# A state space layer's schedule: eight decay tiles, one copy for two, and steps moved by a few turns

## The chip, the cores and the metric

The kernel runs on one core of a Trainium2 chip. The metric is device time in microseconds (us). The core has a matrix engine (TensorE, PE in the profile), a vector engine (VectorE, DVE), an activation engine (ScalarE, ACT), a general engine (GpSimd, POOL) and a queue engine (SyncE, SP) that issues most of the DMAs. Each of them works through its own instructions in their program order, and waits at an instruction until what it needs is there; a weight load (PEld) can run ahead of PE's matmuls.

## The reference, cut to what matters

The whole model is a metaformer of four layers on an input of 4 x 64 x 128 x 128. The change lies in the convolution part of its third layer (layer 2), a state space layer followed by an MLP. For each of 4 batches it sees 64 channels and 8192 positions (image row w, channel c):

```python
xn = layer_norm(xf) over the 64 channels          # mu, var, rsqrt, ln_g, ln_b
xz = in_proj(xn); xi, z = split(xz)               # 128 each
xs = silu(causal_conv4(xi) + conv_b)
dt, Bm, Cm = split(x_proj(xs))                    # 4, 16 and 16 rows
dt = softplus(dt_proj(dt) + dt_proj_b)            # 128 rows
# for every position t, inner channel d and state s of 16:
h[d, s] = exp(dt[t, d] * A[d, s]) * h[d, s] + dt[t, d] * xs[t, d] * Bm[t, s]
y[t, d] = sum_s h[d, s] * Cm[t, s] + xs[t, d] * D[d]
out = out_proj(y * silu(z))                       # 64 channels
# over the last axis of 128:
result = fc2(gelu(fc1(out) + fc1_b)) + fc2_b      # 128 -> 512 -> 128
```

The layer's input is normed once more ahead of it, over the last axis, and its result is added to the input (the residual).

## The kernel before, in words

`l2_conv` (line 2353) goes through 64 **chunks**: two pairs of batches, and in each pair 32 groups of four image columns, L = 512 positions. A chunk has T = 32 **units**: two batches times 16 states. In a unit the 128 partitions hold two states of 64 inner channels, and its work is

- `decay` (ACT, L2821): da = exp(dt * A), one 128 x 512 activation, into one of five buffers;
- `spread` (PE, L2831, once for two units): a matmul with a one-hot matrix repeats two rows of Bm over the partitions, into one of four PSUM banks;
- `inputs` (DVE, L2865): dx * spread rows, into a PSUM bank;
- `one_state` (DVE, L2873): the scan h = da * h + input along the 512 positions; then on POOL (L2878) the product gs with the row of Cm, which DMA has repeated over the partitions (`fetch`);
- `summed` (PE, L2889, for two units, five units later): the sum over the states, accumulated in `py`.

Units 16 and 17 of a chunk are "apart": their da lies in a PSUM bank, and POOL makes their input.

The order on PE, ACT, DVE and POOL is written by hand. A loop runs over **turns** t, one for each unit. A turn emits the decay and the spread of unit t + 3, the input of unit t + 1, the scan of unit t, then all steps that `at(turn, ...)` has put down for this turn, then `summed` of unit t - 5. Each engine keeps this order; SP's order alone is left to the framework. The steps belong to three groups, each with a start turn t0 that is a multiple of 32:

- `norm(n, T * (n - 2))`, the norm over channels of chunk n, two chunks ahead: `scale` (ACT), `centre` (PE, matmul into the bank `pn`, L2544), `square` (ACT: a copy and a square, L2547 and L2548), `mean2` (PE, four matmuls of two columns, L2553), `root` (ACT), `newton` (POOL, four small ones), `back` (PE, 16 matmuls as the trace counts them, L2572), `kept` (ACT, a copy, L2578), `done` (POOL, L2585 and L2586).
- `project(n, T * (n - 1))`, one chunk ahead: `conv` (PE, 4 steps), `conv_out` (ACT, L2630), `gate_in` (PE, L2636), `gate_out` (ACT, L2639), `silu` (ACT with two table loads, L2645 and L2473), `bcr` (PE, x_proj, L2651), `bcr_out` (ACT: bt in bf16, bc and r, L2655 to L2657), `minus` and `part` (PE and ACT, which leave the bf16 rest of Bm in further rows), `steps` (PE, dt_proj, L2677), then softplus: `parts`, `exp`, `one_more`, `log` on ACT, `lost`, `add_lost`, `size`, `scaled` on POOL (L2696 to L2713), and `twice`, DMAs on SP that put dt and dx into the units' layout. `load_res` fetches the residual.
- `leave(n, T * (n + 1))`, the chunk after: `sums` (DVE, L2745), `project_out` and `projected`, `layer1` (PE, L2758), `hidden` (ACT, L2763), `gelu` (ACT with two table loads), `layer2` (PE: bias with a one-row matmul, residual with the identity, then eight products in two steps; L2774 to L2777), `put` (ACT, a copy L2784, and the store), each for the two batches 0 and 1 of the pair.

`centre`, `mean2`, `back`, `project_out` and `layer2` share one PSUM bank, `pn`: each of them waits until the one before has been read. `conv`, `gate_in`, `bcr`, `steps` and `layer1` share the two-bank tile `pa` in the same way. Once in four chunks (`statistics`), DVE takes the first norm's statistics of 16 columns, POOL merges them at turn 24 (v, L2504), ACT takes the root at turn 26 (L2508), and POOL makes rs16 and nb at turn 28 (up to L2520), which `scale` needs at turn 30.

Of the kernel before, what the change touches and what calls it, by code (L numbers as in the profile page):

```python
# [2352 lines left out]
def l2_conv(env, x, out, prm):  # L2353
# [15 lines left out]
    with ExitStack() as ctx:  # L2369
# [7 lines left out]
        def load(name, shape, src):  # L2377
            t = cp.tile(shape, F32, name=name)
            nc.sync.dma_start(t, src)
            return t  # L2380
# [54 lines left out]
        nc.vector.tensor_scalar(minus_i, env.ident[0 : 2 * N, 0 : 2 * N], -1.0, None, ALU.mult)  # L2435
        both = cp.tile([P, H], F32, name="both")
        nc.vector.tensor_add(both, env.ident[:, 0:H], env.ident[:, H:P])
        dtw = load("dtw", [R, D], prm["dt_proj_wT"])
        dtb = load("dtb", [P, 1], prm["dt_proj_b"].unsqueeze(1))
        am = cp.tile([P, S // 2, 2], F32, name="am")  # L2440
        for i in range(2):
# [27 lines left out]
        def at(turn, *steps):  # L2469
            turns.setdefault(turn, []).extend(steps)  # L2470
# [58 lines left out]
        def norm(n, t0):  # L2529
            g, w0 = chunks[n]  # L2530
            x_ = boxes[n]

            def scale(js):
                r, k = x_["rows"]
                if 0 in js:
                    tile_of(x_, "xn", [P, 3 + L], bufs=3)
                for j in js:
                    nc.scalar.activation(
                        x_["xn"][:, 3 + j * C : 3 + j * C + C], r["xt"][:, k + j, :], AF.Identity,
                        bias=r["nb"][:, k + j : k + j + 1], scale=r["rs16"][:, k + j : k + j + 1],  # L2540
                    )

            def centre():
                nc.tensor.matmul(tile_of(x_, "pm", [P, L], "pn", 1, pool=p1), less, x_["xn"][:, 3:], start=True, stop=True)  # L2544

            def square():
                nc.scalar.copy(x_["xn"][:, 3:], x_["pm"])  # L2547
                nc.scalar.activation(tile_of(x_, "sq", [P, L], "sq", 1), x_["pm"], AF.Square)  # L2548

            def mean2():  # L2550
                pv = tile_of(x_, "pv", [P, NW, 2], "pn", 1, pool=p1)
                for q in range(NW):
                    nc.tensor.matmul(pv[:, q, :], x_["sq"][:, q * C : q * C + C], each, start=True, stop=True)  # L2553

            def root():
                v, rs = tile_of(x_, "v", [P, NW, 2]), tile_of(x_, "rs", [P, NW, 2])
                nc.scalar.activation(v, x_["pv"], AF.Identity, bias=env.eps5)
                nc.scalar.activation(rs, v, AF.Ln)
                nc.scalar.activation(rs, rs, AF.Exp, scale=-0.5)

            def newton():
                v, rs, t = x_["v"], x_["rs"], tile_of(x_, "r2", [P, NW, 2])
                nc.gpsimd.tensor_tensor(t, rs, rs, ALU.mult)
                nc.gpsimd.tensor_tensor(t, t, v, ALU.mult)
                nc.gpsimd.tensor_scalar(t, t, 0.5, -1.5, ALU.mult, ALU.add)
                nc.gpsimd.tensor_tensor(rs, rs, t, ALU.mult)

            def back():
                pr = tile_of(x_, "pr", [P, L], "pn", 1, pool=p1)
                for q in range(NW):  # L2570
                    for b in range(2):
                        nc.tensor.matmul(  # L2572
                            pr[b * H : b * H + H, q * C : q * C + C], x_["rs"][:, q, b : b + 1].to_broadcast([P, H]),
                            env.ident, start=True, stop=True,
                        )

            def kept():
                nc.scalar.copy(tile_of(x_, "rt", [P, L], bufs=1), x_["pr"])  # L2578

            def done():  # L2580
                xn = x_["xn"]
                if w0 == 0:
                    nc.gpsimd.memset(xn[:, 0:3], 0.0)
                else:
                    nc.gpsimd.tensor_copy(xn[:, 0:3], boxes[n - 1]["xn"][:, L : L + 3])  # L2585
                nc.gpsimd.tensor_tensor(xn[:, 3:], xn[:, 3:], x_["rt"], ALU.mult)  # L2586

            at(t0 - 2, lambda: scale((0, 1)))
            at(t0, lambda: scale((2, 3)))
            at(t0 + 3, centre)  # L2590
            at(t0 + 4, square)
            at(t0 + 5, mean2)
            at(t0 + 6, root)
            at(t0 + 8, newton)
            at(t0 + 11, back)
            at(t0 + 12, kept)
            at(t0 + 13, done)


        def project(n, t0):  # L2600
# [52 lines left out]
            def bcr_out():  # L2653
                ps = x_["ps"]
                nc.scalar.copy(tile_of(x_, "bt", [3 * N, 2, L], dt=BF16), ps[0 : 3 * N])  # L2655
                nc.scalar.copy(tile_of(x_, "bc", [2 * N, 2, L], bufs=1), ps[0 : 2 * N])
                nc.scalar.copy(tile_of(x_, "r", [R, 2, L], bufs=1), ps[3 * N : 3 * N + R])  # L2657

            def c_out():
                for b in range(2):  # L2660
# [13 lines left out]
            def steps():  # L2674
                pu = tile_of(x_, "pu", [P, 2, L], "pa", 1, pool=pa)
                for b in range(2):
                    nc.tensor.matmul(pu[:, b, :], dtw, x_["r"][:, b, :], start=True, stop=True)  # L2677

            def parts():
                pu = x_["pu"]  # L2680
# [32 lines left out]
                nc.gpsimd.tensor_tensor(x_["dx"], x_["dt"], x_["xs"], ALU.mult)  # L2713

            for k in range(4):
                at(t0 - 8 + k, lambda k=k: conv(k))
            at(t0 - 4, conv_out)
            at(t0 - 2, gate_in)
            at(t0 - 1, gate_out)
            at(t0 + 1, silu)  # L2720
            at(t0 + 7, lambda: bcr(0))
            at(t0 + 8, lambda: bcr(1))
            at(t0 + 9, bcr_out, c_out)
# [15 lines left out]
        def leave(n, t0):  # L2739
# [12 lines left out]
            def projected(b):  # L2752
                nc.scalar.copy(tile_of(x_, "o%d" % b, [P, NW * H], bufs=1), x_["po"].rearrange("c w h -> c (w h)"))
# [11 lines left out]
            def gelu():  # L2765
# [2 lines left out]
                    nc.scalar.activation(gl, gl, AF.Gelu)  # L2768
                base_table()

            def layer2(b, q):
                if q == 0:
                    tile_of(x_, "p2%d" % b, [P, NW // 2, C], "pn", 1, pool=p1)
                    nc.tensor.matmul(x_["p2%d" % b], one_row, b2, start=True, stop=False)  # L2774
                    nc.tensor.matmul(x_["p2%d" % b], env.ident, x_["res%d" % b], start=False, stop=False)
                for k in range(F):
                    nc.tensor.matmul(  # L2777
                        x_["p2%d" % b][:, q, :], x_["gl%d" % b][:, k, q * P : q * P + P], f2[:, k, :],
                        start=False, stop=(q == 1 and k == F - 1),
                    )  # L2780
# [7 lines left out]

            at(t0 - S + LAG, lambda: sums(0))
            at(t0 + LAG, lambda: sums(1))  # L2790
            at(t0 + 9, lambda: project_out(0))
            at(t0 + 10, lambda: projected(0))
            at(t0 + 13, lambda: project_out(1))
            at(t0 + 14, lambda: projected(1))
            at(t0 + 18, lambda: layer1(0))
            at(t0 + 19, lambda: hidden(0))
            at(t0 + 21, lambda: layer1(1))
            at(t0 + 22, lambda: hidden(1))
            at(t0 + 24, gelu)
            at(t0 + 28, lambda: layer2(0, 0))  # L2800
            at(t0 + 29, lambda: layer2(0, 1))
            at(t0 + 30, lambda: put(0))
            at(t0 + 31, lambda: layer2(1, 0))
            at(t0 + 32, lambda: layer2(1, 1))
            at(t0 + 33, lambda: put(1))


        def unit(t):
# [8 lines left out]

        def decay(t):
            x_, b, s, _ = unit(t)
            da = bank(t, t % 2) if apart(t) else sb.tile([P, L], F32, name="da", bufs=5)  # L2820
            nc.scalar.activation(da, x_["dt%d" % b][:, s % 2, :], AF.Exp, scale=am[:, s : s + 1])  # L2821
            live["da", t] = da

# [72 lines left out]
        with tc.manual_schedule(engines={E_.PE, E_.Activation, E_.DVE, E_.Pool}):  # L2896
            base_table()
            for n in range(0, len(chunks), NG):
                statistics(n, T * (n - 3))
            for n in range(len(chunks)):  # L2900
                norm(n, T * (n - 2))
                project(n, T * (n - 1))
                leave(n, T * (n + 1))
            for t in range(-4 * T, units + 2 * T):
                if 0 <= t + 3 < units:
                    decay(t + 3)
                if 0 <= t + 3 < units:
                    if (t + 3) % 2 == 0 and not apart(t + 3):
                        spread(t + 3)
                if 0 <= t + 10 < units and t % 2 == 0 and apart(t + 10):  # L2910
                    fetch_b(t + 10)
                if 0 <= t + 5 < units and apart(t + 5):
                    inputs_apart(t + 5)
                if t % QU == 2 and 0 <= t + 6 < units:
                    fetch(t + 6)
                if 0 <= t + 1 < units and not apart(t + 1):
                    inputs(t + 1)
                if 0 <= t < units:
                    one_state(t)
                for step in turns.pop(t, ()):  # L2920
                    step()
                if 0 <= t - LAG < units and (t - LAG) % 2 == 1:
                    summed(t - LAG)
# [697 lines left out]
```

## Time and profile before

| | us |
|---|---|
| median of 3 runs (lowest, highest) | 10864.77 (10863.57, 10869.84) |
| the profiled execution's own time | 10859.66 |
| its span | 10857.9 |
| this layer's units in the span (first to last scan) | 5992 to 9861 |
| engine busy over the span: PE, DVE, ACT, POOL | 60%, 84%, 66%, 63% |
| granted PE clock, mean | 0.769 |

The profile is of one execution. "Idle before" in a row is the time that the engine stood still ahead of the instruction, with what ended that wait. PEclk is the share of PE's full clock that was granted. Rows of a timeline merge like instructions in succession: start, length, engine, line, operation, tile written <- tiles read, form, count; a matmul in f32 shows as two entries.

### The profile page before, as it was taken

To read this page: it belongs to the slowest core of one execution; us is meant where nothing else is said; L and a number is where in the kernel's file an instruction comes from. 1 tells how busy PE (TensorE), PEld (TensorE's weight loads), DVE (VectorE), ACT (ScalarE), POOL (GpSimd) and SP (SyncE) were. 2 spreads that over 40 slices of the span, in tenths; PEclk is the share of its full clock that TensorE was granted. 3 is DMA by queue.
4 is the path that set the end of the run, shared out by engine and by line. 5 is a ranking of instruction groups with operands and counts; after the bars stand their busy time and mean duration, and the time that the engine had idled before them with its cause. 6 is when DMAs were issued, how large, how long until landed. Compare 5 with 4: busy or idle time off the path is not lost. (4 is left out here: it accounts for less than half of the span.)

```text
span 10857.9 us, 116461 instructions
## 1 busy us (share of the span) xinstructions
PE 6462.2 (60%) x33010; PEld 3787.5 (35%) x33010; DVE 9085.2 (84%) x15515; ACT 7198.7 (66%) x11205; POOL 6797.2 (63%) x6142
## 2 busy tenths in 40 slices
PE   6877777100000000008997888888888888887665
PEld 5665454000000000007886333333333333335342
DVE  7567746899999999997785899999999999996455
ACT  4244453688886888746563788888888888885443
POOL 1000014899996876615553899998999999994322
PEclk8887788555555555559998888888888888888887
DMA  5312135211111222221111444545454545443544
GB/s 196 116 31 48 49 133 174 77 58 58 57 58 52 75 74 72 65 60 46 54 56 41 116 122 124 128 120 124 120 130 120 128 120 131 120 123 103 190 143 168
DMA packets 806505, 1080.45 MB, mean 100 GB/s; under 512 B 245612, under 2 KB 462926, under 8 KB 792270
## 3 DMA queue, kind: packets, MB, share of 16 engines
q1 hardware_dynamic: 761918, 946.59, 31.0%
q0 software_dynamic: 34368, 124.14, 3.4%
q8 instruction: 266, 4.36, 0.2%
q14 instruction: 401, 3.28, 0.1%
q10 hardware_dynamic: 9552, 2.08, 0.1%
HBM read 699.16 MB, written 255.91 MB: 88 GB/s over the span
## 5 line engine op out<-in xcount | busy, mean ns | idle before, releaser
L2878 POOL TENSOR_TENSOR gs<-hist,cc 128x512 f32<-128x512 f32 x2048 | 2572.4, 1274 | 269.3 <-DVE hist L2873 199.3
L2873 DVE TENSOR_TENSOR_SCAN hist<-da,state,bs 128x512 f32<-128x512 f32 x1860 | 2362.6, 1272 | 46.9 <-ACT da L2821 45.7
L1749 PE MATMUL pm<-ident,m 128*1 128x128 f32 x1 | 0.4, 373 | 2846.9 <-DMA pk<-spare 2846.9
L2865 DVE TENSOR_TENSOR bs<-dx,bs 128x512 f32<-128x512 f32 x1920 | 1302.0, 678 | 161.2 <-PE bs L2831 112.1
L1506 POOL TENSOR_TENSOR diff<-key 128x2048 f32<-128x2048 f32 (+11 forms) x364 | 1383.8, 3849 | 82.0 <-DVE key L1511 76.0
L2821 ACT ACTIVATE da<-dt,am 128x512 f32<-128x512 f32 x1920 | 1294.3, 715 | 37.9 <-DVE hist L2873 29.5
L2889 PE MATMUL py<-gs,both 128*64 128x512 f32 x4096 | 1213.8, 672 | 1.4 <-POOL gs L2878 1.3
L1749 PEld LDWEIGHTS pm<-ident,m 128*1 128x1 f32 x1 | 0.1, 79 | 2847.1 <-issue 2847.1
L1504 ACT COPY low<-key 128x2048 f32<-128x2048 f32 (+11 forms) x364 | 627.7, 1725 | 313.8 <-DVE key L1511 276.6
L1567 DVE COPY_PREDICATED rank<-back,rank 128x512 int16<-128x512 int32 (+12 forms) x884 | 815.8, 973 | 3.7 <-POOL both L1554 2.8
L1559 ACT ACTIVATE back<-turned 128x512 int32<-128x512 int8 (+12 forms) x884 | 671.9, 782 | 197.2 <-DVE rank L1569 179.3
L1511 DVE TENSOR_TENSOR key<-low,key 128x2048 f32<-128x2048 f32 (+11 forms) x364 | 744.5, 2045 | 12.4
L1510 DVE TENSOR_TENSOR key<-low,key 128x2048 f32<-128x2048 f32 (+11 forms) x364 | 749.2, 2058 | 2.4 <-ACT low L1504 2.4
L1507 ACT ACTIVATE turned<-diff 128x2048 int8<-128x2048 f32 (+11 forms) x364 | 600.4, 1699 | 8.1 <-POOL diff L1506 8.1
L1554 POOL TENSOR_TENSOR both<-rank 128x640 int32<-128x640 int32 (+12 forms) x156 | 379.6, 2433 | 318.9 <-DVE rank L1569 313.5
L1031 POOL DMA_DIRECT2D state<-zz x16 | 18.5, 1158 | 860.2 <-DVE zz L1021 619.0
L2300 PE MATMUL pe<-ew,xg 128*128 128x128 f32 x4096 | 506.9, 278 | 0.0
L1573 POOL TENSOR_TENSOR rank<-both,rank 128x256 int32<-128x256 int32 (+13 forms) x312 | 422.7, 1376 | 129.2 <-DVE rank L1567 99.1
L2300 PEld LDWEIGHTS pe<-ew,xg 128*128 128x128 f32 x4096 | 491.7, 194 | 19.6 <-issue 3.3
L2831 PE MATMUL bs<-bt,pick 96*128 96x512 bf16 x960 | 394.4, 411 | 122.4 <-DVE hist L2873 119.7
L2758 PE MATMUL pa<-o,f 128*128 128x256 f32 x1024 | 362.4, 515 | 104.9 <-ACT gl L2763 88.9
L1569 DVE COPY_PREDICATED rank<-back,keep 128x512 int16<-128x512 int32 (+14 forms) x416 | 411.4, 989 | 14.2
(860 smaller groups left out, 17974.7 us busy)
## 6 DMA issues: line engine op xcount, KB each, us to landing
cc<-cd SPq DMA_DIRECT2D x1024, 256.0 KB
xt<-state SPq DMA_DIRECT2D x64, 1024.0 KB
dt<-w SPq DMA_DIRECT2D x512, 128.0 KB
dx<-up SPq DMA_DIRECT2D x512, 128.0 KB
xo<-state SPq DMA_DIRECT2D x128, 256.0 KB
state<-xo POOLq DMA_DIRECT2D x128, 256.0 KB, 2.9
xl<-in_L_ffn_weight SPq DMA_DIRECT2D x32, 1024.0 KB
tk<-in_x SPq DMA_DIRECT2D x32, 512.0 KB
```

The lines of the kernel that those rows point to most:

```text
L1504: nc.scalar.copy(c, l)
L1506: nc.gpsimd.tensor_sub(d, lo[part], hi[part])
L1510: nc.vector.tensor_tensor(lo[part], c, hi[part], ALU.min)
L1511: nc.vector.tensor_tensor(hi[part], c, hi[part], ALU.max)
L1559: nc.scalar.activation(m, sv[part], AF.Relu)
L1567: nc.vector.copy_predicated(l, m, h)
L2300: T.matmul(w["pe"][:, j, :], w["xg"][:, q, j, :], ew[:, q, :], start=False, stop=(j == 3 and q == E - 1))
L2821: nc.scalar.activation(da, x_["dt%d" % b][:, s % 2, :], AF.Exp, scale=am[:, s : s + 1])
L2865: nc.vector.tensor_mul(live["db", t], x_["dx%d" % b][:, s % 2, :], live["bs", t - s % 2])
L2873: nc.vector.tensor_tensor_scan(h, live.pop(("da", t)), live.pop(("db", t)), 0.0 if first else state[b][:, s : s + 1], ALU.mult, ALU.add,)
L2878: nc.gpsimd.tensor_tensor(gs, h, live.pop(("cc", t)), ALU.mult)
L2889: nc.tensor.matmul(x_["py%d" % b][h * H : h * H + H], both, live.pop(("gs", t - 1 + h)), start=False, stop=(s == S - 1),)
```

## The change

Five edits, all in `l2_conv`:

- **Eight decay tiles.** `decay` of an ordinary unit is emitted five turns ahead instead of three, with eight buffers instead of five. The apart units keep three turns.
- **Merged copy.** `bcr_out` copies the 100 rows of x_proj's result into `bc` at once, instead of 64 rows into `bc` and 4 into `r`. `steps` then multiplies all 100 rows; dt_proj's weights stand in the last four rows of a 100-row tile, and the others are zero.
- **Later norm.** From `centre` on, the steps go from turns 3, 4, 5, 6, 8, 11, 12, 13 to 5, 7, 9, 10, 12, 15, 16, 18.
- **Gate and silu a turn later**, and with them `conv` and `conv_out`.
- **MLP.** `project_out(0)` and `projected(0)` go two turns later, layer 1 and hidden of batch 1 and gelu one turn, layer 2 and put of batch 1 three turns (put from 33 to 36). The bias and residual matmuls of layer 2 become a step of their own, `kept_sum`, at turn 24 for batch 0 (was 28) and turn 33 for batch 1 (was 31).

```diff
-        dtw = load("dtw", [R, D], prm["dt_proj_wT"])
+        dtw = cp.tile([3 * N + R, D], F32, name="dtw")
+        nc.vector.memset(dtw, 0.0)
+        nc.sync.dma_start(dtw[3 * N :], prm["dt_proj_wT"])
...
-            at(t0 + 3, centre)
-            at(t0 + 4, square)
-            at(t0 + 5, mean2)
-            at(t0 + 6, root)
-            at(t0 + 8, newton)
-            at(t0 + 11, back)
-            at(t0 + 12, kept)
-            at(t0 + 13, done)
+            at(t0 + 5, centre)
+            at(t0 + 7, square)
+            at(t0 + 9, mean2)
+            at(t0 + 10, root)
+            at(t0 + 12, newton)
+            at(t0 + 15, back)
+            at(t0 + 16, kept)
+            at(t0 + 18, done)
...
-                nc.scalar.copy(tile_of(x_, "bc", [2 * N, 2, L], bufs=1), ps[0 : 2 * N])
-                nc.scalar.copy(tile_of(x_, "r", [R, 2, L], bufs=1), ps[3 * N : 3 * N + R])
+                nc.scalar.copy(tile_of(x_, "bc", [3 * N + R, 2, L], bufs=1), ps[0 : 3 * N + R])
...
-                    nc.tensor.matmul(pu[:, b, :], dtw, x_["r"][:, b, :], start=True, stop=True)
+                    nc.tensor.matmul(pu[:, b, :], dtw, x_["bc"][:, b, :], start=True, stop=True)
...
-                at(t0 - 8 + k, lambda k=k: conv(k))
-            at(t0 - 4, conv_out)
-            at(t0 - 2, gate_in)
-            at(t0 - 1, gate_out)
-            at(t0 + 1, silu)
+                at(t0 - 7 + k, lambda k=k: conv(k))
+            at(t0 - 3, conv_out)
+            at(t0 - 1, gate_in)
+            at(t0, gate_out)
+            at(t0 + 2, silu)
...
+            def kept_sum(b):
+                tile_of(x_, "p2%d" % b, [P, NW // 2, C], "pn", 1, pool=p1)
+                nc.tensor.matmul(x_["p2%d" % b], one_row, b2, start=True, stop=False)
+                nc.tensor.matmul(x_["p2%d" % b], env.ident, x_["res%d" % b], start=False, stop=False)
+
             def layer2(b, q):
-                if q == 0:
-                    tile_of(x_, "p2%d" % b, [P, NW // 2, C], "pn", 1, pool=p1)
-                    nc.tensor.matmul(x_["p2%d" % b], one_row, b2, start=True, stop=False)
-                    nc.tensor.matmul(x_["p2%d" % b], env.ident, x_["res%d" % b], start=False, stop=False)
...
-            at(t0 + 9, lambda: project_out(0))
-            at(t0 + 10, lambda: projected(0))
+            at(t0 + 11, lambda: project_out(0))
+            at(t0 + 12, lambda: projected(0))
...
-            at(t0 + 21, lambda: layer1(1))
-            at(t0 + 22, lambda: hidden(1))
-            at(t0 + 24, gelu)
+            at(t0 + 22, lambda: layer1(1))
+            at(t0 + 23, lambda: hidden(1))
+            at(t0 + 25, gelu)
+            at(t0 + 24, lambda: kept_sum(0))
...
-            at(t0 + 31, lambda: layer2(1, 0))
-            at(t0 + 32, lambda: layer2(1, 1))
-            at(t0 + 33, lambda: put(1))
+            at(t0 + 33, lambda: kept_sum(1))
+            at(t0 + 34, lambda: layer2(1, 0))
+            at(t0 + 35, lambda: layer2(1, 1))
+            at(t0 + 36, lambda: put(1))
...
-            da = bank(t, t % 2) if apart(t) else sb.tile([P, L], F32, name="da", bufs=5)
+            da = bank(t, t % 2) if apart(t) else sb.tile([P, L], F32, name="da", bufs=8)
...
-                if 0 <= t + 3 < units:
+                if 0 <= t + 5 < units and not apart(t + 5):
+                    decay(t + 5)
+                if 0 <= t + 3 < units and apart(t + 3):
                     decay(t + 3)
```

## The prediction, made before the changed kernel was run

> **What bounds it now.** I read the page first, then the busy time of the one stage that the diff touches (5992 to 9861 us of the span), then VectorE's waits in it, then the timeline around each wait.
>
> ```profile
> span 10857.9 us, 116461 instructions
> ```
> ```profile
> 5992.00:9861.00 3869.00, 3389.76 (x13423) 1436.10 (x13423) 3693.70 (x4337) 3174.67 (x4770) 3512.25 (x3505) 0.89 0.49 123
> ```
> Columns of the second: window, us, busy us of PE, PEld, DVE, ACT, POOL, then clock and DMA. DVE is busy 3693.7 of 3869 us (95%). It is the bound; all that can be won is its idle rest, 173 us.
> ```profile
> DVE bs L2865 <- PE bs L2831: 112.1, 100, 3.1
> DVE hist L2873 <- ACT da L2821: 46.7, 53, 3.1
> DVE st L2492 <- DMA xt<-state: 12.0, 10, 2.7
> DVE bs L2865 <- DMA dx<-up: 1.5, 2, 1.0
> ```
> So DVE waits for PE's spread (112 us) and ACT's decay (47 us). Counting scans (L2873) from each chunk's first, the waits sit at fixed places. Over 64 chunks: 30.8 us in 19 waits ahead of unit 22's input, 41.7 us in 33 ahead of unit 26's, and the rest around units 1 to 11, mostly in chunks 2, 6, 10, ..., which follow the chunk with the statistics.
>
> (A chunk's kind below is its number modulo 4, so these are kind 2, and kind 1 has the statistics.)
>
> Unit 22: PE's timeline in chunk 26, then two windows of 3.4 us in the columns above, then DVE:
> ```profile
> 7602.48 1.98 PE L2677 MATMUL pa<-r,dtw 4*128 4x512 f32 x4
> 7605.62 0.61 PE L2831 MATMUL bs<-bt,pick 96*128 96x512 bf16 x1
> 7606.68 3.78 PE L2758 MATMUL pa<-o,f 128*128 128x256 f32 x8 [0.44 <-ACT up L2682]
> 7610.39 1.83 PE L2889 MATMUL py<-gs,both 128*64 128x512 f32 x4
> ```
> ```profile
> 7601.70:7605.12 3.42, 3.42 (x13) 0.95 (x9) 3.42 (x4) 1.83 (x3) 3.42 (x5) 1.00 0.26 57
> 7605.12:7608.53 3.41, 2.97 (x7) 1.62 (x6) 3.41 (x5) 3.38 (x5) 3.41 (x5) 0.50 0.48 133
> ```
> ```profile
> 7612.58 0.70 DVE L2865 TENSOR_TENSOR bs<-dx,bs 128x512 f32<-128x512 f32 x1 [1.84 <-PE bs L2831]
> ```
> PE was busy all 3.42 us, yet the clock was halved after it. The window held the four-row matmul of L2677. Layer 1 then took 3.78 us (1.99 at full clock) and DVE waited 1.84. The clock falls like this at units 17 to 19 in 45 chunks.
>
> Unit 26, PE in chunk 24:
> ```profile
> 7488.92 3.68 PE L2758 MATMUL pa<-o,f 128*128 128x256 f32 x8 [2.60 <-ACT gl L2763]
> ```
> PE idles 2.60 us for ACT's hidden(0), the clock drops, layer 1 takes 3.68 us, and the spread behind it is 1.3 us late.
>
> Early units, timeline into chunk 26 (ACT, DVE, PE):
> ```profile
> 7564.96 0.22 ACT L2508 ACTIVATE rs<-v 128x16 f32<-128x16 f32 x1 [4.42 <-POOL v L2504]
> 7571.75 0.88 ACT L2538 ACTIVATE xn<-xt,nb,rs 128x128 f32<-128x128 f32 x2 [2.62 <-POOL nb L2520]
> 7581.88 1.28 DVE L2873 TENSOR_TENSOR_SCAN hist<-da,state,bs 128x512 f32<-128x512 f32 x1 [3.07 <-ACT da L2821]
> 7584.09 1.87 PE L2553 MATMUL pn<-each,sq 128*128 128x2 f32 x8 [5.08 <-ACT sq L2548]
> ```
> ACT waits for POOL's statistics, silu comes late, unit 5's decay is 3.07 us late; PE stands 5.08 us at mean2, and unit 10's input waits 1.29 us more.
>
> **The change, part by part.** A unit at DVE's pace is 1.77 us.
>
> *Merged copy.* ACT loses L2657: 63 x 1.007 = 63 us of an engine that is not the bound. At turns 9 to 13, PE's minus waits for that copy (0.86 us each time), so part, project_out and spread(18) come about 1 us sooner. `back` (16 matmuls, 1.1 us) also leaves that stretch. In chunk 26 spread(18) stood at 7602.16, some 1.9 us after scan 14 allowed it; I take `steps`, parts and what follows as 1.2 us earlier in chunks of kinds 0, 2, 3, and unmoved in kind 1, where spread(18) waited for DVE already.
>
> *The dtw matmul, 100 rows for 4.* Its 0.64 us a piece stays (64 rows: 0.63; 128 rows: 0.70). In the trace only windows with that matmul, with long idle or with the two-column mean2 lose the clock; windows full of 64- to 128-row matmuls never do. So I take the 45 drops as gone: layer 1(0) back to 1.99 us, unit 22's wait closed, **-31 us**. Bounds: 0, if rows of zero weights count as idle, and -31. I take the end whose rows lie nearest, 96 rows (L2831) and 100 columns over 128 rows (L2651). `back`, now between `steps` and layer 1(0), costs 1.1 us of PE; layer 1(0) waited 0.44 us for ACT and starts earlier by the 1.2 us, so it is covered; uncovered, it would put 1.1 us on units 20 to 22.
>
> The Trainium skill ("TensorE: Matmul & The Clock Gate", "What's actually happening") says that how busy PE has been sets the clock. Read plainly, a window busy throughout keeps it, and the widening is worth nothing; the sum would be 31 us less. The window above, 3.42 us of 3.42 and then 0.50, speaks against that reading.
>
> *Unit 26.* `kept` (0.58 us, 0.47 net) now stands on ACT behind parts and ahead of hidden(0). Net hidden(0) is 0.7 us sooner in kinds 0, 2, 3, so PE's 2.60 us idle shrinks to 1.0 to 1.9 us, mostly too little to lose the clock (windows over 0.6 busy kept it). layer1(1) a turn later changes nothing on PE: no instruction lies between. **-30 us** of 41.7. Bounds: -42, and +30 if only the 0.47 us counts (64 x 0.47).
>
> *Decays five units ahead, silu and put(1) later, mean2 two turns behind square.* In kinds 0, 1 and 3 the waits at units 5, 9, 11, 17 and 30 add up to 24 us. A silu with its two table loads holds ACT 4.6 us, 2.6 units; three units of lead did not always cover it, five do. PE's stall at mean2 goes, since square now has two turns. **-22 us**; bounds 0 and -24. Eight tiles cost nothing; decay(t+5) needs scan t-3, long past.
>
> *Chunks 2, 6, 10, ....* Sixteen chunks wait 4.1 us each at units 1 to 11 (66 us). Here `done` (1.09 + 0.15 us) bites: it moves behind `lost` into POOL's stretch without idle, so v and nb come 1.3 us later. From nb, now 7573.0, by the durations above: scale, 2 decays, gate_out, scale, 2 decays: 7578.0; silu 4.6; 2 decays 1.25; put(1) 0.35: 7584.2. The decays reach unit 9 in time, so the 3.07 us goes. But centre shares put(1)'s bank, so PE, done with spread(40) near 7578.3, stands 5.9 us at centre. Behind it are two summed steps and spread(42), which DVE wants at 7585.5. At half clock (2.0 + 4.0 + 0.6 us) it is 5.2 us late, at full clock 2.2. I take 4.3, since the clock returns on the way: **+3 us** for 16 chunks. Bounds: -31 (2.2), +18 (5.2).
>
> *Nothing or little.* kept_sum moves 1.4 us of PE off the critical run into turns 24 and 33; residuals are issued long before (their load stands on SP near unit 5 to 8). If not, PE and all spreads behind it would wait. decay(32) moves two turns up and meets dt's landing (near unit 27, with the 0.7 unit from `done`); ACT arrives at 27.5, conv_out behind it has 1.4 units to spare. On SP the last quarter of dx1 goes behind put(0)'s stores; unit 19 needs it, 15 units on. dx0's first half lands near 29.2, later 29.9, wanted at 30.7. The xt wait (12 us) stays. For what a denser rhythm leaves, **+8 us** (0 to 30).
>
> Sum: -31 -30 -22 +3 +8 = -72 us. Of the profiled execution's own 10859.7 us that leaves 10788; the median of the runs shown is 5.1 us above it: **10793 us**, I write 10792. PE is busy 88% and POOL 91% of the stage; both fit into 3797 us.
>
> **Rivals.**
> 1. *More: the late chunk closes too*, if POOL or ACT catches up and put(1) is in time: the 66 us go instead of +3, and unit 26 entirely: -31 -42 -22 -66 +8 = -153, 10712 us. For it: POOL idles 0.7 us before gs(18). Against: it is saturated from `lost` on. Chance 0.14.
> 2. *The widening does nothing*: zero rows count as idle, the clock falls at units 17 to 19 in every chunk, and the waits at 22 and 26 only trade places as they do now. Left: -22 +3 +8 = -11, 10854 us. Chance 0.12.
> 3. *Slower: centre behind put(1) stalls every chunk.* I have put(1) ending at unit 5.0 of an ordinary chunk. If ACT is 1.6 us (half clock) to 3.4 us (full clock) later, past unit 5.9 to 6.9, spread(42) is late there too. At 3 us in the 48 other chunks: +144 - 72 = +72, 10937 us. For it: ACT carries 4.6 us of gelu, then 4.6 of silu within nine turns. Against: put(1) needs only two decays after silu. Chance 0.10.
>
> **How the numbers follow.** The forecast has 0.64, its own range 10745 to 10835 from the bounds above (all terms rarely meet their ends together). A measurement tells about 0.2%, 22 us, from no change, so faster means under 10843. Faster: 0.62 of the forecast, 0.14, and 0.03 of the second rival: 0.79. Same: 0.02 + 0.07: 0.09. Slower: 0.02 + 0.10: 0.12. The range, 10725 to 10860, takes in the second rival and part of the first; it leaves out the third.
>
> **What would show it.** Right: no half clock at units 17 to 19, layer 1(0) near 2.0 us everywhere, no DVE wait for decays, one 3 to 5 us wait at unit 10 in every fourth chunk with PE idle at L2546 (centre) before it, DVE idle near 100 us. Wrong: L2678 (100 rows) still followed by a 0.50 clock; waits at L2546 in every chunk; waits for dx or dt.

## The result, and the profile after

The change makes the kernel 0.24% slower: 10893.87 us median (10888.19 to 10911.19, 14 runs) beside 10870.81 us for the kernel before on the same chip (14 runs), ratio 1.0024 with a 95% interval of 1.0017 to 1.0032. The forecast was 10792 us. The profiled execution took 10893.31 us; the time outside this layer's units is within 2 us of before, the layer itself took 3900 us instead of 3869.

The page's first line, the window over the layer (window, us, busy us of PE, PEld, DVE, ACT, POOL, clock, DMA), and VectorE's waits in it (total us, times, longest):

```profile
span 10891.5 us, 116126 instructions
```
```profile
5990.00:9891.00 3901.00, 3306.31 (x13433) 1441.81 (x13429) 3679.37 (x4337) 3116.15 (x4708) 3508.59 (x3506) 0.91 0.50 122
```
```profile
DVE bs L2869 <- PE bs L2835: 163.6, 78, 5.8
DVE st L2494 <- DMA xt<-state: 36.1, 13, 5.9
DVE bs L2869 <- DMA dx<-up: 16.7, 17, 1.9
DVE pa L2626 <- PE pa L2620: 1.9, 1, 1.9
```

DVE works 14 us less and stands idle 46 us more. The waits for decays are gone; the waits for the spread rose from 112 to 164 us, in fewer and longer pieces. (Lines moved: decay is L2825, spread L2835, input L2869, scan L2877, the dtw matmul L2678, layer 1 L2759, hidden L2764.) The idle time counted by its place in the chunk, from the traces (us, times):

| DVE idle ahead of | before | after |
|---|---|---|
| unit 5 (decay) | 41.0 us, 45 times | 0 |
| the statistics (xt load) | 12.0, 10 | 36.1, 13 |
| unit 10 | 24.8, 45 | 74.3, 15 |
| unit 20 | 1.0, 2 | 13.6, 20 |
| unit 22 | 30.8, 19 | 0 |
| unit 26 | 41.7, 33 | 76.3, 48 |
| unit 32 (dx0) | 1.0, 1 | 16.2, 16 |
| all | 175 | 221 |

Unit 22: PE's timeline in chunk 24 (the columns are those of the timelines above):

```profile
7483.07 0.38 PE L2835 MATMUL bs<-bt,pick 96*128 96x512 bf16 x1 [2.28 <-DVE hist L2877]
7483.29 1.88 PE L2678 MATMUL pa<-bc,dtw 100*128 100x512 f32 x4
7485.10 1.09 PE L2574 MATMUL pn<-ident,rs 128*64 128x128 f32 x16
7487.44 1.99 PE L2759 MATMUL pa<-o,f 128*128 128x256 f32 x8
```

The matmul with 100 rows is followed by full clock, and layer 1 takes 1.99 us. The first line matters as much: spread(18) stands 2.28 us for scan 14, because it goes into the PSUM bank in which unit 14's input lay. Whatever time PE gains ahead of it is lost there.

Unit 26 in the same chunk: ACT from the first of the two parts (L2682) over kept (L2580) to hidden(0) (L2764), then the first and the last of these in before (chunk 24), then PE and DVE of after:

```profile
7485.26 1.12 ACT L2682 ACTIVATE e<-pa,dtb 128x1024 f32<-128x1024 f32 x1 [1.40 <-PE pa L2678]
...
7487.27 0.59 ACT L2580 COPY rt<-pn 128x512 f32<-128x512 f32 x1
...
7493.77 1.54 ACT L2764 ACTIVATE gl<-pa,b 128x256 f32<-128x256 f32 x4
```
```profile
7479.30 1.11 ACT L2681 ACTIVATE e<-pa,dtb 128x1024 f32<-128x1024 f32 x1 [1.59 <-PE pa L2677]
...
7487.33 1.54 ACT L2763 ACTIVATE gl<-pa,b 128x256 f32<-128x256 f32 x4
```
```profile
7495.37 3.63 PE L2759 MATMUL pa<-o,f 128*128 128x256 f32 x8 [2.49 <-ACT gl L2764]
```
```profile
7501.27 0.70 DVE L2869 TENSOR_TENSOR bs<-dx,bs 128x512 f32<-128x512 f32 x1 [1.15 <-PE bs L2835]
```

This is the picture of before, unmended. With kept in the way, ACT takes 8.51 us from the parts to hidden(0), 8.03 in before. Hidden(0) comes at unit 21.35 of the chunk (21.40 before), PE stands idle 2.49 us ahead of the second layer 1, the clock is halved, layer 1 takes 3.63 us, and spread(26), queued behind it, is 1.15 us late. The late chunk (chunk 26, the first behind the one with the statistics), PE and DVE:

```profile
7596.19 2.08 PE L2546 MATMUL pn<-xn,less_mean 128*128 128x512 f32 x2 [5.83 <-ACT res L2786]
```
```profile
7602.05 0.70 DVE L2869 TENSOR_TENSOR bs<-dx,bs 128x512 f32<-128x512 f32 x1 [4.45 <-PE bs L2835]
```

PE stands 5.83 us at centre for put(1) (5.9 was forecast), and unit 10 waits 4.45 us (4.3 was forecast).

### The profile page after: what moved, and what is told of

Same layout as the page of the kernel before. It is cut to its first block, busy times and chain, and to the rows that moved or that the text cites. A ratio compares the mean times of both kernels' runs of the same rounds, so it can differ in the third digit from the quotient of the medians.

```text
span 10891.5 us, 116126 instructions
## 1 busy us (share of the span) xinstructions
PE 6380.0 (59%) x33010; PEld 3793.7 (35%) x33010; DVE 9072.3 (83%) x15516; ACT 7136.7 (66%) x11141; POOL 6792.6 (62%) x6142
## 5 line engine op out<-in xcount | busy, mean ns | idle before, releaser
L2877 DVE TENSOR_TENSOR_SCAN hist<-da,state,bs 128x512 f32<-128x512 f32 x1860 | 2359.3, 1271 | 0.9 <-issue 0.4
L2869 DVE TENSOR_TENSOR bs<-dx,bs 128x512 f32<-128x512 f32 x1920 | 1298.1, 676 | 222.3 <-PE bs L2835 163.6
L2825 ACT ACTIVATE da<-dt,am 128x512 f32<-128x512 f32 x1920 | 1294.0, 717 | 66.3 <-DMA dt<-w 51.4
L2893 PE MATMUL py<-gs,both 128*64 128x512 f32 x4096 | 1181.5, 646 | 8.0 <-POOL gs L2882 8.0
L2835 PE MATMUL bs<-bt,pick 96*128 96x512 bf16 x960 | 381.4, 397 | 269.7 <-DVE hist L2877 264.1
L2759 PE MATMUL pa<-o,f 128*128 128x256 f32 x1024 | 328.6, 477 | 162.8 <-ACT gl L2764 161.9
```

The source lines that it names most:

```text
L2869: nc.vector.tensor_mul(live["db", t], x_["dx%d" % b][:, s % 2, :], live["bs", t - s % 2])
L2877: nc.vector.tensor_tensor_scan(h, live.pop(("da", t)), live.pop(("db", t)), 0.0 if first else state[b][:, s : s + 1], ALU.mult, ALU.add,)
L2893: nc.tensor.matmul(x_["py%d" % b][h * H : h * H + H], both, live.pop(("gs", t - 1 + h)), start=False, stop=(s == S - 1),)
```

## The experiments

Times of single experiments are compared by their ratios to before, each against runs of before on the same chip; 0.1% is 10.9 us. After stands at 1.0024 in all of them. A sum given for a unit is DVE's idle time in the one profiled run, put down to the unit ahead of which it fell. The letters are those of the theories and rivals in the expectations.

### The rows of the dtw matmul, inside after

```diff
-                    nc.tensor.matmul(pu[:, b, :], dtw, x_["bc"][:, b, :], start=True, stop=True)
+                    nc.tensor.matmul(pu[:, b, :], dtw[3 * N :], x_["bc"][3 * N : 3 * N + R, b, :], start=True, stop=True)
```

> The changed kernel, but the dt projection multiplies only the last 4 of the 100 copied rows (dtw[96:100] with bc[96:100]); everything else, ScalarE's single copy too, stays. Theory S (swap): the half clock only moves. With 4 rows it falls again at units 17 to 19 in over 30 chunks, the wait ahead of unit 22's input comes back (10 to 30 us), the wait ahead of unit 26's input falls from 76 us to under 55 us, and the time stays within 20 us of the changed kernel. Rival G (the full clock is a gain of its own, and the loss comes from elsewhere): unit 22's wait comes back and unit 26's stays near 76 us, so the time grows by 20 to 35 us. Rival Z (rows of zero weights count as idle, the widening did nothing): no change of the clock's places and of the time.

Measured: 10932.14 us, ratio 1.0063 (1.0050 to 1.0076), 42 us above after. Half clock in the layer rose from 683 to 908 us, so rival Z is out. Unit 20 now waits 95 us (60 times), unit 26 only 29, xt 53. So the widened matmul is worth some 42 us in after, and it is not what made after slow. Theory S missed the time and had the wrong unit (20, not 22), but two waits do trade: where the first layer 1 is late, the second waits less for hidden(0).

### The second layer 1 behind the next spread

```diff
-            at(t0 + 22, lambda: layer1(1))
-            at(t0 + 23, lambda: hidden(1))
+            at(t0 + 23, lambda: layer1(1))
+            at(t0 + 24, lambda: hidden(1))
```

> The changed kernel with layer 1 of batch 1 at turn 23 instead of 22, which puts it on TensorE behind spread(26) instead of ahead of it, and hidden(1) at 24 instead of 23. Theory S (unit 26 waits because spread(26) is queued behind a layer 1 that waits for ScalarE's hidden(0) and then runs at half clock): the 76 us of waits ahead of unit 26's input fall under 10 us, TensorE still idles ahead of layer 1 and its clock still falls there, and the time falls by 50 to 76 us, to 10820 to 10845. Rival R (TensorE is simply behind in this stretch, with back and the bias matmuls now in it): the wait moves to unit 28 and the time falls by under 20 us.

Measured: 10872.33 us, ratio 1.0003 (0.9995 to 1.0012), 23 us under after. Unit 26's 76 us are gone, as theory S said, and 6.6 us turned up at unit 28. But the time fell by less than half of the 50 us that it gave at the least, for the wait for dx rose from 17 to 60 us (49 times), probably because nothing ahead of it slows DVE any more:

```profile
DVE bs L2869 <- DMA dx<-up: 60.5, 49, 3.2
```

### `done` a turn earlier

```diff
-            at(t0 + 18, done)
+            at(t0 + 17, done)
```

> The changed kernel with the norm's last step, done (two GpSimd instructions, 1.24 us), at turn 17 instead of 18, which puts it ahead of lost, where GpSimd idles, instead of behind it. Theory P (done behind lost delays all of GpSimd's later steps): waits for dx fall from 16 us to under 4, the statistics' v comes about 1 us sooner and the wait at unit 10 in every fourth chunk falls from 4.6 to about 3.5 us: 15 to 35 us less in all. Rival: done waits there for ScalarE's kept, lost comes no sooner, and the time stays within 10 us.

Measured: 10853.95 us, ratio 0.9990 (0.9981 to 0.9999), 37 us under after. One turn puts `done` ahead of `lost` on POOL again. The dx wait goes (16 to 1.7 us), unit 10's falls from 74 to 44, xt's from 36 to 24.5; unit 26's grows from 76 to 106. Theory P holds.

### The statistics two turns later

```diff
-                at(t0 + 7 + j, lambda j=j: stats(j))
+                at(t0 + 9 + j, lambda j=j: stats(j))
```

> The changed kernel with the 16 statistics instructions of VectorE two turns later (9 to 24 instead of 7 to 22). Theory X (the xt load is issued about 2 us later than before, behind two more dx transfers on SyncE, and the statistics wait for it): the 36 us of waits for xt fall under 8, GpSimd's merge at turn 24 runs after unit 27 anyway and comes no later, and the time falls by 25 to 35 us. Rival: the merge or what follows it comes later, and the wait at unit 10 of every fourth chunk (4.6 us) grows by as much as is saved.

Measured: 10849.21 us, ratio 0.9983 (0.9975 to 0.9992), 45 us under after. The wait for xt is gone, and nothing took its place but 8 us at unit 26. Theory X holds, and the gain is larger than it said:

```profile
DVE st L2494 <- DMA xt<-state: 2.2, 4, 0.9
```

### The logarithm behind hidden(0)

```diff
-            at(t0 + 18, log, lost)
-            at(t0 + 20, load_res, add_lost)
+            at(t0 + 18, lost)
+            at(t0 + 20, load_res, log, add_lost)
```

> After, with ACT's logarithm (L2694, 1.04 us) put behind the first hidden(0) instead of ahead of it. Theory A: unit 26 waits because hidden(0) reaches PE too late, so that PE idles about 2.5 us ahead of the second layer1 and loses its clock. Then that idle shrinks by about 1 us, the 76 us at unit 26 fall to 10 to 40, and the kernel gains 15 to 40 us less whatever the dx wait (16 us now, behind the same logarithm by way of POOL) grows. Rival B: the idle of VectorE is what POOL and PE leave over as a whole, and the wait only changes its place: the sum of VectorE's idle stays within 15 us of 221, and so does the time.

Measured: 10862.65 us, ratio 1.0002 (0.9993 to 1.0011), 24 us under after. PE's wait for hidden(0) ahead of the second layer 1 fell from 160 to 113 us, unit 26's from 76 to 24; the waits at unit 32, behind the same logarithm, rose from 18 to 57. Theory A holds: unit 26 is set by hidden(0)'s place on ACT.

### Before, with the merged copy and the wide matmul alone

```diff
-                nc.scalar.copy(tile_of(x_, "bc", [2 * N, 2, L], bufs=1), ps[0 : 2 * N])
-                nc.scalar.copy(tile_of(x_, "r", [R, 2, L], bufs=1), ps[3 * N : 3 * N + R])
+                nc.scalar.copy(tile_of(x_, "bc", [3 * N + R, 2, L], bufs=1), ps[0 : 3 * N + R])
...
-                    nc.tensor.matmul(pu[:, b, :], dtw, x_["r"][:, b, :], start=True, stop=True)
+                    nc.tensor.matmul(pu[:, b, :], dtw, x_["bc"][:, b, :], start=True, stop=True)
```

(with the 100-row tile of weights, as in the change.)

> Before, with the merged copy and the 100-row dtw matmul alone. Theory A (a gain of its own): the half clock at units 17 to 19 goes, unit 22's 31 us go, unit 26's 42 us grow by 10 to 25 since PE then idles longer ahead of the second layer1, and the kernel is 10 to 25 us faster than before. Rival C (a swap): what unit 22 loses unit 26 takes, 42 us become 70 to 80, and the time is within 10 us of before. Rival D: the slower total of after is this part's: over 10 us slower than before.

Measured: 10809.51 us, ratio 0.9947 (0.9934 to 0.9961): faster by about 57 us, more than any theory gave it. Its DVE waits:

```profile
DVE bs L2866 <- PE bs L2832: 61.0, 64, 2.7
DVE hist L2874 <- ACT da L2822: 52.1, 49, 3.1
DVE st L2494 <- DMA xt<-state: 8.3, 6, 2.5
```

Unit 22's 31 us are gone and unit 26's fell from 42 to 33.5, although PE's wait ahead of the second layer 1 rose from 87 to 114 us. So this one of the five edits is worth 0.5% by itself, and the other four together cost some 80 us.

### Three edits together

The edits of e2, e3 and e4 in one kernel.

> After, with three edits together: the second layer1 and its hidden a turn later, done at turn 17 instead of 18, the statistics two turns later. Alone they took 21, 40 and 45 us from after. Theory A (each wait has its own place and its own cause): the unit 26 wait of 76 us, the xt wait of 36 us and the dx wait of 16 us go, unit 10's 74 us fall to about 44, VectorE's idle is 60 to 100 us, and the time lies 90 to 130 us under after. Rival B (the wait only changes its place): idle stays above 150 us and the time is at most 60 us under after.

Measured: 10776.74 us, ratio 0.9922 (0.9909 to 0.9936), 111 us under after; alone the three had given 23, 37 and 45. They add up, as theory A said: each wait has its own cause. Left are 129 us of idle: unit 10's 63 us (15 times), 21 us at unit 20, 13.5 at unit 28 and 27 at unit 32.

### The three edits and a later centre

```diff
-            at(t0 + 5, centre)
-            at(t0 + 7, square)
+            at(t0 + 7, centre)
+            at(t0 + 8, square)
```

> The kernel of the three edits, with centre two turns later and square one turn later (turns 7 and 8), so that spread(42) and the summed steps stand ahead of centre on PE. Theory A: the unit 10 wait of every fourth chunk is PE standing at centre for put(1); it goes (44 to 74 us become under 15), and the time falls a further 30 to 60 us if nothing behind mean2 is late. Rival B: square and mean2, with newton behind them on POOL, come too late for the gelu and conv that follow, and VectorE waits at units 25 to 32 instead: the time is within 15 us of the kernel of the three edits, or above it.

Measured: 10703.53 us (10698.24 to 10712.58), ratio 0.9854 (0.9840 to 0.9867): 73 us less than e7, 1.46% faster than before. PE's timeline in chunk 26, then DVE's waits:

```profile
7513.44 0.61 PE L2835 MATMUL bs<-bt,pick 96*128 96x512 bf16 x1
7513.85 1.91 PE L2653 MATMUL pa<-xs,xp 128*100 128x512 f32 x2
7515.55 1.09 PE L2546 MATMUL pn<-xn,less_mean 128*128 128x512 f32 x2
```
```profile
DVE bs L2869 <- PE bs L2835: 43.3, 70, 2.7
DVE bs L2869 <- DMA dx<-up: 11.2, 19, 1.9
```

Spread(42), which is unit 10's in the next chunk, now goes ahead of centre. Centre no longer waits, unit 10 never does, and all idle is 56 us.

### The later norm and second half undone

After, with the norm's steps, the first project_out and layer 2 of batch 1 with its put back at before's turns (those of the change's diff; the split-off `kept_sum(1)` goes to turn 30).

> After, with the norm's eight steps, the first project_out and the second half of layer 2 with put(1) back at before's turns; what stays of the change is the merged copy, eight decays five ahead, conv, gate and silu a turn later, layer1(1) a turn later and the split-off bias. Theory A (the later norm is what turned a gain into a loss, through kept ahead of hidden(0), done behind lost, and put(1) ahead of centre): unit 26's 76 us fall to 25 to 45, unit 10's 74 to under 35, the dx wait to under 5, xt's 36 to about 12, and the time is 10760 to 10820 us. Rival E (the decays five ahead and the later silu are the cost): unit 26 and unit 10 stay above 50 us each and the time is over 10860.

Measured: 10959.5 us, ratio 1.0088 (1.0074 to 1.0102), 70 us **above** after: theory A was wrong on the time. PE's timeline in an ordinary chunk:

```profile
7491.38 1.87 PE L2555 MATMUL pn<-each,sq 128*128 128x2 f32 x8 [3.87 <-ACT sq L2550]
```

With silu a turn later and the norm not, square stands behind silu on ACT, PE stands at mean2 in every chunk, and units 2, 4 and 10 wait 38, 50 and 148 us (about 60 times each). The later norm is what the later silu needs. One part of A held: without kept ahead of hidden(0), unit 26 waits 31.6 us.

### The merged copy and the eight decay tiles

Before with the edit of e6 and the decays' part of the change's diff.

> Before, with the merged copy and the 100-row dtw matmul, and eight decay tiles, five units ahead; every turn as before. Theory A (five units of lead cover silu): unit 5's wait of 48 us goes, unit 10's 23 us grow to 25 to 45, and the time is 10 to 45 us under that of the merged copy alone (10809). Rival F (the late chunk is late whatever the lead): all of unit 5's wait turns up at unit 10, and the time is within 10 us of 10809.

Measured: 10808.4 us, ratio 0.9948 (0.9935 to 0.9962), the same as e6. Unit 5's 48 us go, unit 10's rise from 23 to 78. Rival F holds: here the lead is worth nothing, since the late chunk loses the same time at PE.

### 36 rows

The merged kernel of e6, with the matmul on rows 64 to 99 of both operands.

> Before with the merged copy, but the dtw matmul takes rows 64 to 99 of it: 36 rows, of which 32 meet zero weights, at the same number of columns and matmuls. Theory A (the clock goes by how many of the array's rows work, with some threshold between 4 and 64): if 36 rows are enough no window full of work is followed by a halved clock, unit 22 waits under 3 us and the time is within 10 us of 10809; if not, half clock returns at units 17 to 19 and the time is 15 to 50 us longer. Rival H (the gain of the merged copy is the copy that ACT saves, not the rows): half clock returns or not, the time is within 10 us of 10809.

Measured: 10817.64 us, ratio 0.9957 (0.9942 to 0.9972), within the spread of e6. The clock fell again ahead of the first layer 1, and unit 22 waits 6.4 us. Half clock at units 15 to 18 took 61 windows of 3.41 us (17 in e6). The clock falls in part, and the time is not told apart from e6's: rival H's time, not the 15 to 50 us of theory A.

### `kept` twice

```diff
                 nc.scalar.copy(tile_of(x_, "rt", [P, L], bufs=1), x_["pr"])
+                nc.scalar.copy(x_["rt"], x_["pr"])
```

> After, with kept's copy (0.59 us, 0.47 net of overlap) issued a second time behind the first, ahead of hidden(0) on ACT. Theory A (unit 26 waits for hidden(0), and kept's place on ACT sets it): PE's idle ahead of the second layer1 grows from about 2.5 to 3.0 us, unit 26's 76 us to 95 to 115, and the time by 15 to 40 us. Rival J (the wait is set by the halved clock alone, which falls in 48 of 64 chunks already): unit 26 grows by under 10 us, and the time is within 12 us of 10894.

Measured: 10979.65 us, ratio 1.0094 (1.0080 to 1.0108), 76 us above after, twice to five times what theory A gave. Unit 26 waits 196 us (60 times). PE's wait for hidden(0) ahead of layer 1, in four kernels: before, the merged copy alone, after, and kept twice (total us, times, longest):

```profile
PE pa L2758 <- ACT gl L2763: 87.2, 50, 2.8
```
```profile
PE pa L2759 <- ACT gl L2764: 114.4, 62, 2.7
```
```profile
PE pa L2759 <- ACT gl L2764: 160.2, 62, 3.3
```
```profile
PE pa L2760 <- ACT gl L2765: 220.1, 62, 3.9
```

From after to kept twice, ACT's stretch from the parts to hidden(0) grows from 8.51 to 9.13 us (median), 38 us in 62 chunks. PE waits 60 us more and unit 26 120 us more. Over the four kernels unit 26 goes 42, 34, 76, 196. The steep end is not the copy alone: in kept twice the dtw matmul itself ran at a lower clock in 38 of 64 chunks (its four entries over 2.5 us; 20 in after, 6 in e6), so the parts came later too.

### Conv, gate and silu a turn earlier again

After, with `conv` to `silu` at before's turns.

> After, with conv, gate and silu back at before's turns, one earlier; the norm stays late. Undoing the late norm alone made the kernel 66 us slower than after, with PE 3.9 us idle at mean2 in each chunk (square stood behind the later silu). Theory K (silu a turn later is the cost that the late norm only repairs): the time is 40 to 100 us under after. Rival L (with the norm late the place of silu no longer matters, the loss lies in kept, done and the statistics): the time is within 20 us of after, and unit 26 keeps over 55 us. Rival M (conv then comes too early for done): waits of over 40 us for conv, gate or the decays behind silu appear, and it is slower than after.

Measured: 10891.02 us, ratio 1.0023 (1.0014 to 1.0032): after's time. Unit 10 falls from 74 to 52 us and xt from 36 to 27, units 2 and 20 take 27 more. Rival L holds: with the norm late, silu's place is worth nothing here.

### `back` and `kept` a turn earlier

```diff
-            at(t0 + 15, back)
-            at(t0 + 16, kept)
+            at(t0 + 14, back)
+            at(t0 + 15, kept)
```

> After, with back and kept one turn earlier, so that kept stands on ACT ahead of the two parts, where ACT idled about 1.4 us for the dtw matmul, instead of between the parts and hidden(0). Kept twice had raised unit 26 from 76 to 196 us. Theory A: hidden(0) comes 0.2 to 0.5 us sooner, unit 26's 76 us fall to 20 to 50 and the time by 20 to 50 us. Rival N (PE's 1.1 us of back now stand ahead of spread(18) and the dtw matmul, and push all of it out again): unit 26 stays at 60 us or more, or units 18 to 20 take 30 us or more, and the time is within 15 us of after.

Measured: 11008.49 us, ratio 1.0138 (1.0123 to 1.0154), 124 us above after. PE's timeline in chunk 24:

```profile
7516.20 1.97 PE L2574 MATMUL pn<-ident,rs 128*64 128x128 f32 x16 [3.14 <-POOL rs L2568]
```

`back` came ahead of spread(18) and stood there for newton on POOL, which runs between two and three units after its turn (from unit 14.5). Unit 18 waits 84 us, dx 51, unit 26 92. The place that ACT has free for kept is one where PE has none for back; rival N's mechanism holds, at a price far over the 15 us it gave.

### The best kernel with silu back, and with five decays

The kernel of e8, once with `conv` to `silu` at before's turns, once with five decay tiles and a lead of three.

> The kernel of the three edits and the later centre (10703.5 us, idle 56 us), with conv, gate and silu at before's turns. Theory K: what silu costs is gone from it too, and it gains 10 to 40 us. Rival L: with the waits mended the place of silu is worth nothing; within 12 us of 10704.

Measured: 10752.98 us, ratio 0.9902 (0.9887 to 0.9917), 52 us above e8: 78 us of wait at unit 28 (58 times), beside 5 us in e8. In this kernel the later silu and conv are worth 52 us; both theories missed.

> The kernel of the three edits and the later centre, with five decay tiles and a lead of three units as before. Beside the merged copy alone the eight tiles were worth nothing: unit 5's 48 us went and unit 10's rose by 55. Theory A (there the late chunk's centre took what the lead gave; here centre no longer holds the spreads, so the lead is worth unit 5's wait): 30 to 60 us slower than 10704, with 25 to 60 us of decay waits near units 2 to 6. Rival F (the lead is worth nothing anywhere): within 12 us of 10704.

Measured: 10731.93 us, ratio 0.9878 (0.9863 to 0.9893), 26 us above e8 by the ratios (the two intervals touch), with 8 us of decay waits at unit 6 and 22 us (35 times) at unit 29; unit 28 took 11 us more, other waits fell, and all idle rose by about 11. The lead is worth some 26 us once centre has left the late chunk: theory A's sign, just under its lower end, and mostly at another unit than it said.

### The merged copy, four rows

The merged kernel of e6, with the matmul on rows 96 to 99 alone.

> Before with the merged copy, and the dtw matmul on rows 96 to 99 of it alone: the copy is saved, the rows are four as before. Rows 0 to 99 gave 10809.5 us, rows 64 to 99 10817.6. Theory A (the rows are the gain): half clock at units 17 to 19 as in before, unit 22 waits 25 to 45 us, and the time is 10840 to 10870. Rival H (the copy saved on ACT is the gain, through the parts and spread(18) coming sooner): the time is 10805 to 10830 whatever the clock does.

Measured: 10823.89 us, ratio 0.9958 (0.9944 to 0.9971). PE's timeline in chunk 26, and PE's wait ahead of the second layer 1:

```profile
7577.15 1.98 PE L2678 MATMUL pa<-bc,dtw 4*128 4x512 f32 x4
...
7581.34 3.78 PE L2759 MATMUL pa<-o,f 128*128 128x256 f32 x8
```
```profile
PE pa L2759 <- ACT gl L2764: 58.2, 56, 2.4
```

The clock falls as in before and unit 22 waits 36 us, but unit 26 only 10 (33.5 with full clock). So theory A had the clock right and rival H the time. The saved copy is worth about 45 us of the 57. What the rows add here, about 12 us, lies within the two intervals; the profiles show why it is little: most of what unit 22 loses comes back at units 26 and 5 (23 and 20 us).

All in one table (DVE's idle time by place, us; unit 32 with all its waits, not dx alone):

| kernel | ratio | unit 10 | unit 26 | xt | unit 32 | all idle |
|---|---|---|---|---|---|---|
| before | 1 | 25 | 42 | 12 | 1 | 175 |
| e6 merged | 0.9947 | 23 | 34 | 8 | 2 | 126 |
| e17 merged, 4 rows | 0.9958 | 18 | 10 | 9 | 0 | 137 |
| e10 merged, decays | 0.9948 | 78 | 44 | 15 | 2 | 150 |
| after | 1.0024 | 74 | 76 | 36 | 18 | 221 |
| e7 three edits | 0.9922 | 63 | 0 | 0 | 27 | 129 |
| e8 and centre | 0.9854 | 0 | 0 | 0 | 23 | 56 |

## Why the prediction was wrong, step by step

**The step that failed is unit 26**: -30 us forecast, +35 measured. It held that hidden(0) would come 0.7 us sooner net of kept and that PE's idle would shrink to 1.0 to 1.9 us. The lead of 1.2 us upstream did not arrive: spread(18) moved only from unit 15.45 to 15.12 in the chunk shown, 0.6 us, then met scan 14 (2.28 us of idle), a limit that the text set for kind 1 alone. In e6 spread(18) meets the same limit at 15.11, so the rest of the change brought it no further. And kept took most of what was left: from the parts to hidden(0) ACT takes 8.02 us on the median in before, e6 and e9, and 8.51 in after. So in chunk 24 hidden(0) came at unit 21.14 in e6 and at 21.35 in after, for 21.40 in before (medians of all chunks 21.14, 21.35 and 21.22), while PE, now at full clock, was ready for it earlier. Its idle there grew (median 2.49 us, 2.01 before; over 2.2 us in 57 of 63 chunks, 16 before). The bound given, +30 if only the 0.47 us counts, came nearest. That ACT's queue ahead of hidden(0) sets this wait is shown by e5 and e12, and by unit 26 itself: 34 and 32 us in e6 and e9, where kept is at before's turn, 76 in after.

**The clock** was right as a mechanism: four rows lose it, 100 rows with 96 of zero weights keep it, and unit 22's wait went, 31 us as forecast. As a term of the sum it was too good: with four rows the merged kernel (e17) has 11 us more idle than with 100 (e6), not 31. The second rival's sentence, that the waits at 22 and 26 trade places, was largely true of these two kernels, which have kept elsewhere; inside after the rows were worth some 42 us.

**The merged copy's own gain** was put into unit 26 and nowhere else; e17 shows about 45 us for the copy alone in before's order: unit 26 falls from 42 to 10, unit 5 from 41 to 27. The change had this gain and lost the part at unit 26 again where kept now stands. No run takes kept alone out of the way: e14 moved `back` with it and lost 124 us.

**xt** ("stays"): +24. In after the load of the next statistics' input is issued on SP at unit 4.6 of the chunk on the median, 3.1 before; the last DMAs of dx1 and put(0) are ahead of it, later than they were. The prediction followed that shift for dx1's last quarter and did not carry it to the xt load behind. e4, which makes the statistics wait for it two turns later, took 45 us off; which of the two DMAs holds it was not tried.

**dx0 and unit 20** (within "+8"): about +28 (unit 32 +15, unit 20 +13). The slack of 0.8 unit that the text gave dx0 was too small for the scatter; e3 shows that `done` behind `lost` is the cause of the dx wait; unit 20 fell only from 14 to 8 us there, and its cause stays open.

**Right:** the decays' waits are gone, at unit 5 (41 us) and beside it; so is PE's stall at mean2 (some 160 us before); the late chunk, +3 forecast for 16 chunks and +9 measured, where unit 5's time reappeared at unit 10 with PE 5.83 us at centre. What went unsaid is that it could be avoided: centre two turns later took it away (e8). The third rival, centre stalling every chunk, did not happen on DVE: PE did stand at centre in 58 chunks (135 us), but in the ordinary ones within its slack.

The decays and the late chunk together (units 1 to 5, 10 and the small ones) gave about -10 us where -22 and +3 stood. Sum of the misses: 65 (unit 26) + 24 (xt) + 20 (dx0 and unit 20, above the 8) + 9 (decays and late chunk), less the 14 us that DVE worked less: 104 of the 106 us between -72 and the +34 of the profiled executions.

## To carry to other kernels

When a moved step lands on another engine's queue, follow the first consumer behind it to its own other condition: a lead is worth nothing past the next wait for the bottleneck (here spread(18) for scan 14), and a small cost just ahead of a wait can grow, by the slow clock behind it and by what is queued there (here 0.62 us more on ACT made 1.4 us more of PE idle in the median chunk, and 76 us in all). Try the parts of a bundled change by themselves; here one line of ACT work was worth about 45 us, one turn 37, and the bundle with four edits to its turns is 1.46% faster than before. A part that is worth nothing now (the decays' lead in e10, silu's place in e13) can be worth 26 or 52 us once the wait beside it is gone.

## What the runs showed of the hardware

How many rows a matmul uses counts for PE's clock, at about the same length of the matmul (0.63 to 0.68 us apiece in the four kernels of the table). In the profiles the clock changes at multiples of 3.41 us alone; such a stretch is a window here. The table takes the layer's windows that PE began at full clock, by the share in which it was busy, and says after how many of them the next had half clock.

| dtw matmul | busy 0.9 and more | busy 5/6 and more |
|---|---|---|
| 4 rows (before) | 39 of 588 | 44 of 625 |
| 4 rows, merged copy (e17) | 19 of 606 | 39 of 646 |
| 36 rows, merged copy (e11) | 0 of 594 | 16 of 637 |
| 100 rows, merged copy (e6) | 0 of 589 | 0 of 633 |

E17, e11 and e6 differ in the rows alone, and rows that meet zero weights count. In after (100 rows) it was 0 of 618 at 5/6 and more. In e1, four rows inside after's order, it was 0 of 577 too, and there the falls at units 14 to 16 came in less busy windows (between 3/4 and 5/6 busy: 18 of 87; 3 of 69 in after). So rows and busy time seem to be weighed together; that weighing was only read off, not measured alone, and rows of weights and rows of data were not told apart. The Trainium skill ("TensorE: Matmul & The Clock Gate", "What's actually happening") makes the clock a matter of how busy PE has been; read plainly that would leave out what the row counts do here.
